# Where the last up sum of two feed-forward columns is kept: in its PSUM bank or in SBUF

## The chip, the core and the metric

The kernel runs on one core of one Trainium2 chip. The metric is the time of one execution on the device, in microseconds (us); of several runs the median is taken. One execution more was taken with the hardware profiler, and all views quoted here are of such executions. The engines are called PE (TensorE, the matmuls), DVE (VectorE), ACT (ScalarE), POOL (GpSimd) and SP (SyncE, which issues the DMAs).

## What is computed

The reference is two layers of cross attention and a feed-forward part each, on x of 8 x 128 tokens and 512 features. The change lies in the last feed-forward part, a gated one with quantised weights:

```python
gate_proj = dequantize(gate_w, gate_s, gate_z, GROUP_SIZE, dt)   # 512 x 1792
up_proj = dequantize(up_w, up_s, up_z, GROUP_SIZE, dt)           # 512 x 1792
down_proj = dequantize(down_w, down_s, down_z, GROUP_SIZE, dt)   # 1792 x 512
gate = jax.nn.silu(jnp.dot(x, gate_proj))
up = jnp.dot(x, up_proj)
return jnp.dot(gate * up, down_proj)
```

`dequantize` subtracts a zero point and multiplies by a scale; both are given for each group of 128 rows and each column. x is normalised before this part, and its result is added to x.

## The kernel before

**The columns.** The 1792 inner features are cut into 14 columns of 128. The list ORDER (line 1089) gives their order: 5, 1, 6, 2, 7, 3, 8, 4, 9, 10, 11, 12, 13, 0. The 1024 tokens are two halves of 512. For columns 0 to 4 the first half of the gated product has been computed ahead, in the layer before, so that only the second half is left here: their instructions are 512 wide, those of the others 1024.

**One column.** Gate and up each have four units (`unit`, line 990), one for each group of 128 rows. A unit is matmuls on PE into a tile f of the PSUM pool `ps_f`, then one instruction that multiplies f by the group's scale and adds it to a sum. [...] The first unit of a sum is a scaled copy on ACT (line 1001). The others are a `scalar_tensor_tensor` on DVE (L1010: the tile `gate` or `up` in SBUF gets f times the scale plus itself). One up unit is different: the fourth, where the whole sum is kept in one tile (`one`, line 1022; all columns but the first three of ORDER). It goes to L1003, which writes the finished sum into f itself, in PSUM, and returns f. In the first three columns the up sum is made of two sums in SBUF, which POOL adds (L1036), and the product reads it there.

Then come `silu` on ACT (L1042), the gated product on DVE (`gated`, L1047: th gets th times the up sum), a rounded copy h_h on ACT (`cast`, L1054) and the remainder h_l = th - h_h (`rest`, L1061). The remainder is made by POOL, in column 0 by DVE (`late`, line 1012). PE multiplies h_l and h_h by the down weights: four units for each column, whose results are summed in `acc`. Such a sum is either L1010 on DVE, or a scaled copy to a tile tmp on ACT (L1007) and an add of two SBUF tiles on POOL (L1008).

**What sets the order.** Most of the kernel is ordered by a scheduler. For the feed-forward part line 1094 (`emit`) gives the program order of a column, and the down units of a column are written among the gate and up units of the next. The last stretch, from line 1122 on, is under `manual_schedule`: on PE, DVE, ACT and POOL the written order is kept. It begins with the product of column 13, the last but one of ORDER; the eight gate and up units of column 0 follow, with the down units of column 12 among them, then the product, cast and remainder of column 0, the down units of column 13, the transposes that turn `acc` back (`turn`, L1159), and the last down units. The fourth up unit of column 13 is still emitted by the loop (line 1120). Each engine takes its instructions in order, and a unit on PE waits until a buffer of `ps_f` is free, that is until the last reader of the tile that held it is done. For an up sum kept in f this last reader is the product.

## Time and profile before

| what | value |
|---|---|
| median of 3 runs | 840.97 us (840.44 to 841.06) |
| the profiled execution | 839.52 us |
| its span, from the first instruction to the last | 837.7 us |
| granted TensorE clock | 1.000 of full speed |
| busy over the span | PE 820.4, DVE 629.9, POOL 598.4, ACT 516.9 us |
| DVE from 797 to 809 us | 11.04 of 12.00 us busy |
| DVE from 809 us to the end | 20.37 of 29 us busy |
| POOL from 809 us to the end | 23.01 of 29 us busy |
| L1047 with the up sum in PSUM | 11 times, 1.21 to 1.22 us (1024 wide), 0.68 to 0.69 us (512 wide) |
| L1047 with the up sum in SBUF | 3 times, 1.61 and 2.17 us (1024 wide), 0.68 us (512 wide) |

Lines of the views read so: start in us, length in us, engine, source line, operation, output<-inputs by the program's names, shapes (partitions x elements), how many were merged; in square brackets the idle time before it and what ended it. In the chain of work that ended last, each piece is start, length and what ran; "issue" is time in which the engine waited for nothing that the profile shows, or, where two instructions overlap in the records, the part of the earlier one that the chain does not follow.

### The profile page before, as it was taken

How to read it: one execution, taken by the hardware profiler on the slowest of the kernel's cores; microseconds unless marked ns; L12 is line 12 of the kernel's file. 1: busy time of each engine (PE TensorE's matmuls, PEld its weight loads, DVE VectorE, ACT ScalarE, POOL GpSimd, SP SyncE). 2: the span in 40 equal slices, each digit the busy share in tenths (PEclk: the TensorE clock that was granted, in tenths of full speed). 3: DMA queues.
4: the chain of work that ended last, by engine and by line, in shares of the span. 5: the costliest groups of instructions: out<-in, count | busy, mean ns of one | idle time of the engine just before them, and what ended most of it. 6: DMA issues, size and time to landing. Idle time of an engine off the chain costs nothing.

```text
span 837.7 us, 14168 instructions
## 1 busy us (share of the span) xinstructions
PE 820.4 (98%) x4312; PEld 694.1 (83%) x4312; DVE 629.9 (75%) x1061; ACT 516.9 (62%) x1694; POOL 598.4 (71%) x612
## 2 busy tenths in 40 slices
PE   7999999999999999999999999999999999999996
PEld 6889998898888888888888888888888877778774
DVE  6805897675777777777777777776798888998996
ACT  6524442245667766776767767676777778665663
POOL 3713882235678888878878778798886678787797
PEclk9999999999999999999999999999999999999999
DMA  9523532173888888898889888888976512221202
GB/s 320 131 69 107 184 114 88 59 240 134 277 248 283 285 280 270 268 282 284 263 271 287 253 279 271 295 265 264 290 241 227 182 58 82 87 84 63 63 27 100
DMA packets 153564, 164.96 MB, mean 197 GB/s; under 512 B 15632, under 2 KB 94224, under 8 KB 153488
## 3 DMA queue, kind: packets, MB, share of 16 engines
q1 hardware_dynamic: 153488, 164.06, 61.2%
q8 instruction: 34, 0.56, 0.3%
q14 instruction: 42, 0.34, 0.1%
HBM read 104.78 MB, written 59.24 MB: 196 GB/s over the span
## 4 chain that ended last, share of the span: by engine, by line
PE 85%; DVE 6%; issue 4%; POOL 3%; ACT 1%; DMA 0%; DVEq 0%; SPq 0%; POOLq 0%; ACTq 0%
PE mm L78 9%; PE mm L80 9%; PE mm L79 9%; PE f L996 7%; PE f L997 7%; PE s L575 7%; PE o L644 6%; PE o L647 6%; PE o L645 6%; PE kv L78 3%; PE kv L80 3%; PE kv L79 3%; PE o L623 2%; PE o L624 2%; PE o L625 2%
## 5 line engine op out<-in xcount | busy, mean ns | idle before, releaser
L589 ACT ACTIVATE pr<-s,nm 128x128 f32<-128x128 f32 x256 | 90.4, 364 | 47.3 <-DVE nm L583 47.1
L616 POOL TENSOR_TENSOR pT_l<-pT,pT_h 128x512 fp32r<-128x512 f32 x64 | 82.9, 1295 | 34.8 <-ACT pT_h L615 23.1
L78 PE MATMUL mm<-wq_l,xnT_h 128*128 128x512 f32 x256 | 105.6, 412 | 0.2 <-DVE q L544 0.2
L80 PE MATMUL mm<-wq_h,xnT_l 128*128 128x512 f32 x256 | 101.2, 395 | 0.0
L79 PE MATMUL mm<-wq_h,xnT_h 128*128 128x512 f32 x256 | 100.7, 393 | 0.0
L644 PE MATMUL o<-wo_l,aT_h 128*128 128x512 f32 x256 | 100.1, 391 | 0.1
L645 PE MATMUL o<-wo_h,aT_h 128*128 128x512 f32 x256 | 99.7, 389 | 0.0
L601 DVE STREAM_TRANSPOSE pb<-pr 128x512 f32<-128x512 f32 x64 | 45.5, 711 | 52.6 <-POOL pr L597 52.6
L597 POOL TENSOR_TENSOR pr<-pr,rs 128x512 f32<-128x512 f32 x64 | 67.9, 1060 | 21.5 <-DVE rs L595 21.2
L535 ACT ACTIVATE junkq<-mm 128x128 f32<-128x128 f32 x256 | 71.6, 280 | 10.9 <-PE mm L80 4.8
L78 PE MATMUL kv<-wkv_l,cT_h 128*128 128x256 f32 x256 | 73.6, 288 | 0.0
L80 PE MATMUL kv<-wkv_h,cT_l 128*128 128x256 f32 x256 | 72.9, 285 | 0.0
L79 PE MATMUL kv<-wkv_h,cT_h 128*128 128x256 f32 x256 | 72.9, 285 | 0.0
L615 ACT CAST pT_h<-pT 128x512 fp32r<-128x512 f32 x64 | 39.8, 622 | 51.7 <-DMA pT<-p_d 50.4
L575 PEld LDWEIGHTS s<-kT,qT 128*128 128x128 f32 x512 | 66.9, 191 | 5.2
L647 PE MATMUL o<-wo_h,aT_l 128*128 128x512 f32 x256 | 69.0, 391 | 0.0
L673 POOL TENSOR_TENSOR qT<-qT,q 128x512 fp32r<-128x512 f32 x42 | 54.0, 1287 | 20.1 <-ACT qT L672 20.1
L366 POOL TENSOR_TENSOR rrq<-msq,nhalf 128x4 f32<-128x4 f32 x64 | 64.5, 1007 | 5.3
L575 PE MATMUL s<-kT,qT 128*128 128x128 f32 x512 | 67.4, 275 | 0.0
L644 PEld LDWEIGHTS o<-wo_l,aT_h 128*128 128x128 f32 x256 | 48.1, 188 | 11.3 <-issue 0.9
L80 PEld LDWEIGHTS mm<-wq_h,xnT_l 128*128 128x128 f32 x256 | 48.1, 188 | 11.0
L629 ACT CAST aT_h<-o 128x512 fp32r<-128x512 f32 x64 | 37.4, 585 | 31.4 <-PE o L625 31.1
(251 smaller groups left out, 2486.8 us busy)
## 6 DMA issues: line engine op xcount, KB each, us to landing
q_d<-qb SPq DMA_DIRECT2D x64, 256.0 KB, 4.3
qT<-q_d SPq DMA_DIRECT2D x64, 256.0 KB, 4.3
p_d<-pb SPq DMA_DIRECT2D x64, 256.0 KB, 2.5
pT<-p_d SPq DMA_DIRECT2D x64, 256.0 KB, 4.5
wst<-in_qpT SPq DMA_DIRECT2D x36, 256.0 KB, 4.2
wst<-in_opT SPq DMA_DIRECT2D x36, 256.0 KB, 3.1
wkv<-in_kvT SPq DMA_DIRECT2D x8, 512.0 KB, 4.0
v_d<-vh SPq DMA_DIRECT2D x16, 256.0 KB, 2.1
```

What stands on the lines that cost most here:

```text
L78: nc.tensor.matmul(o, ah, bl, start=start, stop=False)
L79: nc.tensor.matmul(o, ah, bh, start=False, stop=False)
L80: nc.tensor.matmul(o, al, bh, start=False, stop=stop)
L366: nc.gpsimd.tensor_tensor(r[:, :n], ms[:, :n], nhalf[:, :n], ALU.pow)
L535: nc.scalar.activation(junk, qps[u][:, r * HD : (r + 1) * HD], AF.Square, accum_out=ssq[:, r : r + 1])
L575: nc.tensor.matmul(sp[:, r, :], qTs[u][:, r, :], kTt[blocks[j]][:, :, i, :], start=True, stop=True)
L589: nc.scalar.activation(pr[:, r, :], sps[u][:, r, :], AF.Exp, bias=nms[u][:, r : r + 1], accum_out=sm[:, r : r + 1])
L597: nc.gpsimd.tensor_tensor(pr, pr, rs.unsqueeze(2).to_broadcast([P, NQ, P]), ALU.mult)
L616: nc.gpsimd.tensor_tensor(pl, tps[u], f32(ph), ALU.subtract)
L644: nc.tensor.matmul(po, ah[:, r, :], wl, start=r == 0, stop=False)
L645: nc.tensor.matmul(po, ah[:, r, :], wh, start=False, stop=False)
L647: nc.tensor.matmul(po, al[:, r, :], wo[wset[j], r][0], start=False, stop=r == NREP - 1)
```

## The change

The condition that sends an up unit to L1003 gets one more clause:

```diff
         upf[c] = unit(
-            "P" if one and (m, g) == ("up", KT - 1) else "V", wfs[m], g, lambda hf: (xn2[hf][0][:, g, :], xn2[hf][1][:, g, :]),
+            "P" if one and (m, g) == ("up", KT - 1) and c not in ORDER[-2:] else "V", wfs[m], g, lambda hf: (xn2[hf][0][:, g, :], xn2[hf][1][:, g, :]),
             s_sb[:, c, g : g + 1], gu[m, a], g == a, (1,) if c < NE else (0, 1),
         )
```

In columns 13 and 0 the fourth up unit is now L1010 like the second and third: it writes the sum into the tile `up` in SBUF. `unit` returns nothing, so `gated` (L1047) takes its up operand from `up` and not from f. The nine other columns with one up sum keep L1003. The order of instructions on each engine is the same before and after; two instructions of DVE have another output, two another second input, and the bank of f is released by the sum and no longer by the product.

## The prediction

> **What bounds the kernel where the change acts.** I read four views, in this order. First the page's fourth part, the chain that ended last: over the whole span it is TensorE's (PE).

> ```profile
> PE 85%; DVE 6%; issue 4%; POOL 3%; ACT 1%; DMA 0%; DVEq 0%; SPq 0%; POOLq 0%; ACTq 0%
> ```

> A mean over 837.7 us says little of the last 30. So, second, the same chain piece by piece from 797 us on. Its columns are start, length and what ran.

> ```profile
> 811.22 1.29 DVE f L1003
> ...
> 812.61 0.09 DVE th L1047
> ...
> 813.75 0.76 DVE gate L1010
> ...
> 820.01 0.77 DVE f L1003
> ...
> 820.87 0.70 DVE th L1047
> ...
> 821.59 0.63 ACT h_h L1054
> ...
> 822.24 0.70 DVE h_l L1061
> 822.95 2.55 POOL acc L1008 x2
> 825.54 0.78 PE f L1159 x5
> ```

> Up to 810.0 us the chain is PE's; from there to 821.57 it is VectorE's (DVE), with both gated products (L1047) in it, and then it runs through ScalarE (ACT), DVE and GpSimd (POOL) into the output. Third, DVE's timeline: from 811.22 to 821.56 its eleven instructions have durations of 1.284, 1.221, 0.746, 0.750, 0.750, 1.274, 0.741, 1.274, 0.740, 0.758 and 0.689, 10.23 us in 10.34. DVE is full there, so what is added to one of its instructions arrives at the end, and what is taken from PE does not. Fourth, the timeline of POOL beside DVE, for what runs while the two products run:

> ```profile
> 812.57 2.38 POOL L1008 TENSOR_TENSOR acc<-acc,tmp 128x1024 f32<-128x1024 f32 x1
> 812.61 1.22 DVE L1047 TENSOR_TENSOR th<-th,f 128x1024 f32<-128x1024 f32 x1
> ...
> 819.84 2.38 POOL L1008 TENSOR_TENSOR acc<-acc,tmp 128x1024 f32<-128x1024 f32 x1
> ...
> 820.87 0.69 DVE L1047 TENSOR_TENSOR th<-th,f 128x512 f32<-128x512 f32 x1
> ```

> Both products run beside a POOL add on SBUF operands and neither notices: one operand is f, in PSUM.

> **The change, part by part.** It replaces no instruction by more or fewer. In columns 13 and 0 the last up sum goes from L1003 (into f) to L1010 (into up), and L1047 reads up. The order on all five engines stays, SP's and its DMAs' with it.

> (1) *The sum itself.* L1003 takes 1.284 us for 1024 columns and 0.751 for 512; L1010 into up 1.281 and 0.747. The gap from the sum to the product that needs it is 0.11 us (811.22 + 1.28 to 812.61), and between two dependent sums into up, in SBUF, it is 0.10 (806.918 + 1.284 to 808.307). Cost: 0.

> (2) *The PSUM bank.* f comes free when the sum ends and no longer when the product ends. PE waited for the products twice, 1.4 us in all:

> ```profile
> PE f L996 <- DVE th L1047: 1.4, 2, 0.7
> ```

> Both go. The third gate sum's matmuls would follow the second's (812.81 + 0.23) at about 813.0 rather than 813.89, but DVE reaches them only at 815.45; behind them PE waits at 814.55 for the bank of the second gate sum, which DVE releases. At 821.71 PE's next step, 822.85, waits for ACT's tmp, behind the same product. So late next is DVE in the one case and ACT in the other, and the gain is 0. Its bounds are 0, and 1.4 us if DVE were not full.

> (3) *The product's second operand.* Now both operands are in SBUF. Before has three such products, in columns 5, 1 and 6. The short one ran while POOL was idle, a long one while POOL was not:

> ```profile
> 699.62 0.68 DVE L1047 TENSOR_TENSOR th<-th,up 128x512 f32<-128x512 f32 x1
> ...
> 709.80 1.32 POOL L1036 TENSOR_TENSOR gate<-gate,gate 128x512 f32<-128x512 f32 x1
> 710.03 2.17 DVE L1047 TENSOR_TENSOR th<-th,up 128x1024 f32<-128x1024 f32 x1
> ```

> Undisturbed it costs what the PSUM form costs (0.68 against 0.69), so the floor of this part is 0. The disturbed one ended at 712.20, 1.08 after POOL's add (711.12); alone the form would take 1.22. So DVE stood until POOL was 0.14 short of its end, then ran whole. The other long one, at 696.34, gives 697.95 - 696.88 = 1.07. A third row, in the next fence, agrees: 686.35 + 1.77 = 688.12, 0.55 after POOL's 687.57, and 0.55 = 0.69 - 0.14. It goes the other way too: POOL's 512 add at 696.82, behind the product that ended at 697.95, took 2.29 instead of 1.30 and ended 1.16 after it, 1.30 - 0.14. I take it as a rule of this trace: of a DVE operation with two SBUF inputs and a POOL operation on SBUF, whoever is first runs alone, the other starts 0.14 before its end.

> [...]

> *Who is first at 812.6?* The POOL add starts at 812.57 and the product asks at 812.61; neither start depends on the change. So POOL leads by 0.04 us. The nearest rows: POOL won with a lead of 0.07,

> ```profile
> 686.28 1.29 POOL L1086 TENSOR_TENSOR h_l<-the,h_h 128x512 fp32r<-128x512 f32 x1
> 686.35 1.77 DVE L740 TENSOR_TENSOR the<-the,qb 128x512 f32<-128x512 f32 x1 [1.18 <-ACT gate L1001]
> ```

> and DVE won with a lead of 0.01 (L66 at 107.35 took its 0.40, POOL's L62 at 107.36 took 1.55 instead of 1.29). The lead of 0.04 is nearer to the row that POOL won, so I take POOL as first.

> Then the first product ends at 814.95 + 1.08 = 816.03, not 813.83: **+2.20**. Queued behind it on DVE, without a gap, are three gate sums, two down sums and three up sums, then the second product: all 2.20 later. ACT's cast (813.87) waits for the product, POOL's remainder (L1061, 814.99) for the cast, and POOL's next two adds follow it: 817.19, 819.57, 822.04. The second product asks at 820.87 + 2.20 = 823.07, while POOL's second add runs from 822.04 to 824.42. It stands again and ends at 824.42 + 0.55 = 824.97, not 821.56: **+3.41**. From there the chain in the second fence has no slack: cast, remainder, two POOL adds, transposes, output. The remainder (822.24) already has two SBUF inputs and a free POOL, as before. Sum: 0 + 0 + 3.41.

> The profiled execution took 839.52 us (span 837.7 and 1.8 around it); it would take 842.9. The median of the runs, 840.97, lies 1.45 above that execution; the same 3.4 on it gives **844.4 us**. Bounds of the unknown cost: 0 if POOL is never in the way, and 2 x (2.38 - 0.14) = 4.5 us, 845.5, if each product stood for a whole add.

> **Rivals.**
> (a) *DVE takes the first collision*, because a start in the trace is not quite the moment of the claim. For it: the lead is only 0.04. Then the first product is on time and POOL's add ends at 813.83 + 2.24 = 816.07. POOL's remainder, first and second add follow at 816.02, 818.39 and 820.74, back to back. The second product asks at 820.87, now 0.13 behind, and stands until 823.12: it ends at 823.67, +2.11. That gives 843.1. If DVE won this as well, POOL's add would end at 823.80 and the remainder, asking at 822.24, at 824.35 rather than 822.94: +1.4, 842.4.
> (b) *Nothing moves*: the POOL adds leave the product alone, both last 1.22 and 0.69, and PE's waits were hidden anyway. For it: both products are covered in before. Against it: five rows in (3). 841.0.
> (c) *Faster*: PE's waits were the limit, not DVE. Then the two 0.69 us of (2) and the 0.44 behind the second (PE at 822.85) go, 1.8 us: 839.2. It decides only if DVE has slack of that size between 811.22 and 821.56; the sum above leaves 0.11, so this is nearly excluded.

> **How the numbers follow.** Forecast 55%, (a) 28% with one collision lost and 6% with none, (b) 7%, (c) 2%, and 2% for more than the forecast. The time is the forecast's, 844.4. The range leaves out (b) and (c): from the lower case of (a), 842.4, to 845.2, which is the forecast and most of the way to the upper bound of 845.5. A measurement of this kernel can tell about 0.2% from no change, 1.7 us, so slower begins at 842.65. Forecast, first case of (a), the excess and half of its second case make 88% for slower; the other half and (b) make 10%; (c) is 2%.

> **What would show it.** Right: L1047 near 812.61 lasts about 3.4 us and ends 1.08 after a POOL add; L1047 near 823.1 lasts about 1.9; L1003 is gone from the last two columns; PE's two waits for th are gone from the list of waits and the span is 3.4 longer all the same. For (a): the first L1047 lasts 1.22, the POOL add beside it 3.5, and the second L1047 2.8. Wrong: both products at 1.22 and 0.69, or an end that moves less than the second product does; then there was slack behind DVE that I have not seen.

## The result, and the profile after

The changed kernel takes 847.94 us (median of six runs, 846.11 to 850.86); the kernel before took 840.8 beside it. The ratio is 1.0084 [1.0059, 1.011], that is 5.0 to 9.2 us more, where 3.4 were forecast and 4.2 were the end of the range. The profiled execution took 850.86 us with a span of 849.1.

That execution is the slowest of the six, and it is already 5.17 us late (816.39 against 811.22) where the changed stretch begins, although the program up to there is the same. Such a drift came with the kernel before's own program too: at the same point the other profiled executions of this study stand at -0.3 (e8) to +6.0 us (e6) against before, and the program of e6 up to there is that of before. One profile, of e2, was of a disturbed execution and was taken again (e9). Profiles are compared by their **tail**: from the start of column 13's last up sum to the end of the span. Before: 837.73 - 811.22 = 26.51 us. After: 849.08 - 816.39 = 32.69, 6.18 more. (The spans of the tails are taken from the traces to two decimals; the views show one.)

The chain that ended last, the first view, is of no use here. Its shares over the whole span:

```profile
PE 70%; DVE 8%; POOL 6%; DMA 6%; issue 6%; ACT 3%; SPq 1%; DVEq 0%; POOLq 0%; ACTq 0%
```

PE's share fell by 15 points, from some 712 to some 594 us, where the two spans differ by 11.4: the chain takes another way far ahead of the change, through waits for DMAs from 223 us on that before's chain does not have. What the change did has to be read from its own stretch. The timeline of DVE in the changed kernel:

```profile
816.39 1.28 DVE L1010 SCALAR_TENSOR_TENSOR up<-f,su_sb,up 128x1024 f32<-128x1024 f32 x1
817.77 3.41 DVE L1047 TENSOR_TENSOR th<-th,up 128x1024 f32<-128x1024 f32 x1
...
826.37 1.28 DVE L1010 SCALAR_TENSOR_TENSOR acc<-f,sd_sb,acc 128x1024 f32<-128x1024 f32 x1 [0.96 <-PE f L997]
...
829.67 2.01 DVE L1047 TENSOR_TENSOR th<-th,up 128x512 f32<-128x512 f32 x1
832.37 0.69 DVE L1061 TENSOR_TENSOR h_l<-th,h_h 128x512 fp32r<-128x512 f32 x1 [0.69 <-ACT h_h L1054]
```

and that of POOL (x3 stands for three adds merged, of which the last is the one beside the first product):

```profile
814.00 6.10 POOL L1008 TENSOR_TENSOR acc<-acc,tmp 128x1024 f32<-128x1024 f32 x3
...
828.75 2.38 POOL L1008 TENSOR_TENSOR acc<-acc,tmp 128x1024 f32<-128x1024 f32 x1 [1.69 <-ACT tmp L1007]
```

The sum lasts what it lasted, and the product follows it after 0.10 us. The first product takes 3.41 us for 1.22 and ends at 821.18, 1.08 after POOL's add (820.10). The second takes 2.01 for 0.69 and ends at 831.68, 0.55 after POOL's add (831.13). So both products stood behind POOL, as forecast. But 2.19 and 1.32 are 3.51 of the tail's 6.18. Between the products DVE now waits for PE (the row at 826.37: 0.96 us), where before it had no such wait. The rest shows on PE, in its timeline:

```profile
821.90 0.50 PE L996 MATMUL f<-h_l,wf_down 128*128 128x512 f32 x1 [3.08 <-DVE gate L1010]
824.36 0.63 PE L996 MATMUL f<-h_l,wf_down 128*128 128x512 f32 x1
...
832.98 0.50 PE L996 MATMUL f<-h_l,wf_down 128*128 128x512 f32 x1 [2.58 <-ACT tmp L1007]
```

PE stood for 3.08 and 2.58 us, and soon after the first stand matmuls took 0.63 us, where those of before take 0.39 to 0.40 (from 816.55 to 818.84 us, at full clock). The same time cut into stretches says why. Columns: stretch, its length, busy us (and count) of PE, PE's weight loads, DVE, ACT and POOL, the granted TensorE clock, DMA share, GB/s:

```profile
819.87:823.28 3.41, 1.38 (x6) 1.04 (x6) 3.20 (x4) 2.06 (x2) 1.17 (x2) 1.00 0.00 0
823.28:826.70 3.42, 3.42 (x10) 2.69 (x9) 2.46 (x4) 1.21 (x3) 3.42 (x2) 0.50 0.00 0
...
830.11:833.52 3.41, 0.83 (x4) 0.30 (x2) 2.73 (x3) 1.79 (x3) 1.48 (x2) 1.00 0.00 0
833.52:836.94 3.42, 3.42 (x11) 2.70 (x11) 2.02 (x4) 1.37 (x2) 3.42 (x4) 0.50 0.00 0
```

Twice PE was idle for most of a stretch of 3.41 us (2.03 and 2.58), and in the stretch behind it the clock was 0.50. In the profile of before the clock is 1.00 until 0.7 us before the end of the span, when PE has long been done. The tail's 6.18 us fall into four parts: first product +2.19; from its end to the start of the second, 8.49 for 7.04 us, +1.45; second product +1.32; from its end to the end of the span, 17.40 for 16.17, +1.22 (and -0.01 ahead of the first).

**Theory A**: the forecast's collisions are there, and by making DVE late they make PE idle so long that its clock falls to half, twice, for 1.45 and 1.22 us. **Theory B**: the clock is a by-product without a price, and the missing 2.7 us come from somewhere else in the changed columns (the drift ahead, another wait). A third question is whether anything but POOL's adds is at work at all.

### The profile page after: what moved, and what is told of

It is laid out like the page before. It is cut to its first block, busy times and chain, and to the rows that moved or that the text cites. A ratio compares the mean times of both kernels' runs of the same rounds, so it can differ in the third digit from the quotient of the medians.

```text
span 849.1 us, 14167 instructions
## 1 busy us (share of the span) xinstructions
PE 824.5 (97%) x4312; PEld 696.4 (82%) x4312; DVE 632.9 (75%) x1061; ACT 517.5 (61%) x1694; POOL 598.7 (71%) x612
## 4 chain that ended last, share of the span: by engine, by line
PE 70%; DVE 8%; POOL 6%; DMA 6%; issue 6%; ACT 3%; SPq 1%; DVEq 0%; POOLq 0%; ACTq 0%
PE f L996 8%; PE f L997 7%; PE mm L78 7%; PE mm L80 7%; PE mm L79 7%; PE o L644 5%; PE o L647 5%; PE o L645 5%; PE s L575 5%; DMA pT<-p_d 3%; PE kv L78 2%; PE kv L80 2%; PE kv L79 2%; DMA q_d<-qb 2%; PE o L623 1%
## 5 line engine op out<-in xcount | busy, mean ns | idle before, releaser
L1008 POOL TENSOR_TENSOR acc<-acc,tmp 128x1024 f32<-128x1024 f32 (+1 forms) x23 | 49.4, 2160 | 13.1 <-ACT tmp L1007 11.0
```

## The experiments

### e3: PE kept busy

The changed kernel, in which two units on PE repeat their matmuls into the same tile just where PE stood. Nothing else is changed.

```diff
...
+            for _ in range(1 + again):
-            nc.tensor.matmul(ps[:, hf, :], w, rl, start=True, stop=False)
-            nc.tensor.matmul(ps[:, hf, :], w, rh, start=False, stop=True)
+                nc.tensor.matmul(ps[:, hf, :], w, rl, start=True, stop=False)
+                nc.tensor.matmul(ps[:, hf, :], w, rh, start=False, stop=True)
...
+            6 if (m, g, c) == ("gate", 3, ORDER[-1]) else 0,
...
+            5 if (o, c, hs) == (2, ORDER[-2], (0,)) else 0,
```

> The changed kernel, with the last gate unit of column 0 multiplied six times more and one down unit of column 13 (third of its first half) five times more, into the same bank with the same result: 22 matmuls that fill 2.7 and 2.3 us of PE's two long waits and wait for nothing. Theory A: both products last as in the changed kernel, 3.4 and 1.9 us, but the clock stays at full speed; the tail is 26.5 + 2.2 + 1.2 = 29.9 us, 2.8 less than in the changed kernel, although PE does more; time 3.4 over before, about 844. Theory B (the 2.8 us are not the clock's): the tail stays at 32.7 or grows by the added matmuls.

Measured: 844.57 us beside 841.02 of before, ratio 1.0037 [1.002, 1.0054], and a tail of 29.98 (841.41 - 811.43), 3.47 longer than before's. With 22 matmuls more the kernel is 3.4 us nearer to before than the changed one (median against median). DVE's timeline and two stretches of e3 (the product is L1049 there):

```profile
812.82 3.46 DVE L1049 TENSOR_TENSOR th<-th,up 128x1024 f32<-128x1024 f32 x1
...
823.31 1.91 DVE L1049 TENSOR_TENSOR th<-th,up 128x512 f32<-128x512 f32 x1
```

```profile
811.40:824.00 12.60, 12.21 (x52) 9.09 (x52) 12.08 (x12) 5.08 (x6) 10.22 (x6) 1.00 0.05 17
824.00:841.00 17.00, 10.82 (x58) 7.76 (x57) 9.99 (x14) 5.42 (x9) 10.65 (x9) 1.00 0.34 124
```

Both collisions are there in full, the clock is 1.00, and DVE's last instruction ends 3.47 later than in before. This is the forecast's case as it was worked out (3.41), and it speaks for A: what lies above it goes with the clock. The mean granted clock of the runs says the same beyond the one profile. One step of 3.41 us at half takes 0.0020 off the mean of such a span, and its end, where PE has nothing left to do, took 0.0004 (before) and 0.0011 (after). The six runs of the changed kernel have 0.997 once, 0.995 four times and 0.993 once: one, two and three such steps. The twelve of e3 have 0.998 to 1.000, so at most one each, and eight of them, at 0.999 or 1.000, none.

### e1, e2, e9: each column alone

The new clause for one column only: in e1 for column 13, in e2 and e9 (the same program) for column 0.

```diff
-... and c not in ORDER[-2:] else "V"
+... and c != ORDER[-2] else "V"
```

> The last up sum goes to SBUF in column 13 alone; column 0 keeps it in f. Compared is the tail, from the start of column 13's last up sum to the end of the span: 26.5 us in the kernel before (811.22 to 837.7), 32.7 in the changed one (816.39 to 849.1). Theory A (the product and POOL's adds exclude each other, and the long wait that this makes on PE lets the granted TensorE clock fall to half for one window): the first product lasts 3.4 us, +2.2; PE then idles some 3.2 us and the clock falls once, +1.4; the second product lasts 0.69. Tail about 30.1, time some 3.6 over before. Theory B (the products are slower by the lock, but the rest of the loss, 2.8 us, comes from elsewhere: PE running ahead on the freed bank, or the weights): no drop of the clock here, tail 28.7. Theory C (the loss belongs to column 0): tail 26.5.

> The last up sum goes to SBUF in column 0 alone; column 13 keeps it in f. The tail is 26.5 us in the kernel before, 32.7 in the changed one. Theory A: the first product lasts 1.22; the second asks at the time it had before, one us into POOL's add of 2.38, and lasts 1.9, +1.2. PE, with its bank free early, then waits some 2.8 us for ACT's tmp; if the granted clock falls for that, +1.3 more. Tail 27.7 without the fall, 29.0 with it; time 1.2 to 2.5 over before. Theory B (PE running ahead on the freed bank costs by itself): the loss is there without a drop of the clock. Theory C (the loss belongs to column 13): tail 26.5.

> The last up sum goes to SBUF in column 0 alone, once more, for its profile. Theory A, as sized by the runs so far: the first product lasts 1.22; the second asks at 9.64 us from the start of column 13's last up sum, beside the POOL add of 8.62 to 11.00, lasts about 1.9 and ends near 11.5 (10.34 before), +1.2; PE then waits 2.5 us, from about 10.4 to 12.9. The clock falls only if a window of 3.41 us holds about two thirds of that wait: the end is 1.2 later than before, or about 2.5.

Measured for column 13 alone: 845.13, ratio 1.0042 [1.0024, 1.0059], tail 31.32 (+4.81). The product takes 3.417 us, 2.20 more, so 2.61 are left. Its stretches:

```profile
816.36:819.78 3.42, 1.19 (x6) 0.67 (x4) 3.32 (x2) 0.00 (x0) 2.40 (x2) 1.00 0.00 0
819.78:823.19 3.41, 2.56 (x6) 2.08 (x7) 2.67 (x5) 2.06 (x2) 2.12 (x1) 0.50 0.00 0
823.19:826.60 3.41, 3.41 (x9) 2.64 (x9) 2.03 (x3) 1.21 (x2) 2.60 (x2) 0.50 0.00 0
```

After a stretch with 2.23 us idle the clock fell, and behind the next one, which still had 0.85 idle, it stayed down for one more. Expected were 30.1 by A and 28.7 by B; A had one stretch at half clock in it.

For column 0 alone: 843.09, ratio 1.0014 [0.9999, 1.0029], not clear of no change. The profile is e9's: tail 28.89 (+2.38). The product takes 1.915 us (+1.23), and DVE's last instruction ends 2.36 later, of which 1.14 come after the product. The mean clock of this profile is 0.997, which by the numbers above is one step at half and the end of the span. That last part does not come in every execution: of the twelve other runs of e2 five have 0.997 too (843.25 to 845.39 us), while four have 0.999 (841.16 to 843.09) and so no step at half clock. The limit that was expected at two thirds of a wait of 2.5 us lies, by the runs, between 1.78 (e4, no fall) and 1.86 us of a step (e11, a fall). The two columns' parts do not add up (4.81 + 2.38 against 6.18): e1's and e9's profiles have three steps at half clock between them, that of the changed kernel two.

### e6, e7: without the two adds

Two POOL adds, of down units (3, 11) and (2, 12), the ones beside the products, are left out: in e6 of the kernel before, in e7 of the changed one.

```diff
...
-            nc.gpsimd.tensor_tensor(dst, dst, a2, ALU.add)
+            if not leave:
+                nc.gpsimd.tensor_tensor(dst, dst, a2, ALU.add)
...
+            (o, c) in ((3, ORDER[-4]), (2, ORDER[-3])),
```

> The kernel before without the two POOL adds that run beside the two products (down sums of column 11, third unit, and column 12, fourth unit, are not added to acc). This is the base for the next run. All theories: the products last 1.22 and 0.69, as before, and POOL has pauses in place of the adds; POOL's last four adds start as before, after the remainder of column 0. Time as before, 841, or up to 0.5 less.

> The changed kernel without the same two POOL adds. Theory A (the whole loss is the exclusion by these two adds and what follows from it): both products last 1.22 and 0.69, PE's waits for the products are gone, the clock stays, and the time is that of the base run within 0.3 us: the early release of the bank is worth nothing, since DVE is full. Theory B (the change costs by itself, by its operands or by PE running ahead): several us over the base remain. Theory C (PE's two waits were worth something): 0.7 to 1.4 us below the base.

Measured: e6 841.68, 1.0012 [0.9996, 1.0029], tail 26.51; e7 841.4, 0.9998 [0.9983, 1.0013], tail 26.52. DVE's products in e7:

```profile
816.86 1.23 DVE L1048 TENSOR_TENSOR th<-th,up 128x1024 f32<-128x1024 f32 x1
...
825.11 0.69 DVE L1048 TENSOR_TENSOR th<-th,up 128x512 f32<-128x512 f32 x1
```

Without these two adds the change neither costs nor gains: the whole difference hangs on the two collisions, and the bank that comes free early gains nothing (the two tails differ by 0.02 us).

### e8: POOL busy, but not reading

The changed kernel, in which the two adds are replaced by memsets of tmp.

```diff
...
-            nc.gpsimd.tensor_tensor(dst, dst, a2, ALU.add)
+            if leave:
+                nc.gpsimd.memset(a2, 0.0)
+            else:
+                nc.gpsimd.tensor_tensor(dst, dst, a2, ALU.add)
```

> The changed kernel with the same two POOL adds replaced by POOL memsets of the same 1024 columns into tmp, which write SBUF and read nothing (the sums are not added to acc). The first memset is under way when the first product asks. Theory A1 (only POOL's reading excludes the product): both products last 1.22 and 0.69, the time is that of the run without the adds. Theory A2 (any POOL instruction on SBUF excludes it): the first product waits for the rest of the memset, some 0.5 to 1.0 us, and the end moves with it.

Measured: 840.13, 0.999 [0.998, 1.0], tail 26.52. The timeline of POOL and DVE:

```profile
812.12 0.95 POOL L1009 MEMSET tmp<- 128x1024 f32 x1
812.29 1.23 DVE L1050 TENSOR_TENSOR th<-th,up 128x1024 f32<-128x1024 f32 x1
...
819.52 0.95 POOL L1009 MEMSET tmp<- 128x1024 f32 x1
```

The product starts 0.17 us after the memset, runs beside it for 0.78, and takes its 1.23. This POOL instruction, which only writes SBUF, does not hold it up; the adds, which read it, do (3.41 us in the profile after). The second memset had run 0.95 us and ended at 820.47, before the product came at 820.55.

### e4, e5: POOL made late

If the first add comes after the first product, DVE should win and POOL stand, the rival (a) of the prediction. A small POOL instruction ahead of the add is to make it late: 128x1 in e4, 128x128 in e5.

```diff
...
+            if late_add:
+                nc.gpsimd.tensor_tensor(fa.tile([P, 1], F32, name="gap"), a2[:, 0, 0:1], a2[:, 0, 0:1], ALU.add)
```

> The changed kernel with one POOL instruction of one column added ahead of the POOL add that starts 0.04 us before the first product, so that this add comes some 0.1 to 0.2 us later and after the product. Theory A, with the order of asking deciding: the first product lasts 1.22 to 1.4, the POOL add 3.5; POOL's next three follow late, the last of them from about 0.1 before the second product asks, so that this one lasts 2.8; the tail is 26.5 + 2.1 = 28.6, and 29.9 if PE's one long wait (3.5 us) lets the clock fall. The changed kernel has 32.7. Theory B (the slow product is not a matter of who is first, but of sharing): the first product lasts 3.4 as in the changed kernel and the tail stays at 32.7.

> As the run before it, with a longer POOL instruction in front (128 columns, some 0.45 us), so that the POOL add cannot start before the first product asks. Times are from the start of column 13's last up sum. Theory A (whoever asks first runs alone, and the one who waits comes next): the first product asks at 1.38, waits at most for the short instruction and lasts 1.2 to 1.3; the POOL add beside it lasts 3.3 to 3.5 and ends near 4.9; POOL's next three follow without a pause, the last starts near 9.5, just ahead of the second product (9.70), which therefore lasts 2.8 and ends near 12.5 (10.34 in the kernel before). The end comes 2.1 later than before, 3.5 if PE's wait of some 3.4 us lets the clock fall; time 843.1 to 844.5. Theory B (a product with two SBUF inputs is slow beside POOL whoever is first): the first product lasts 3.3 again and the end stays 5 to 6 later.

e4 did not do what it was for: the add came 1.263 us after the start of the up sum, where it comes 1.35 after it in the kernel before, so POOL won again and the product took 3.327. It took 848.53, 1.0077 [1.0055, 1.01], tail 31.39. It is of use for another reason. In its profile PE's second stand is spread over two stretches, so that this one follows the first fall:

```profile
826.54:829.96 3.42, 1.64 (x7) 0.98 (x6) 2.76 (x2) 0.46 (x1) 2.38 (x1) 1.00 0.00 0
829.96:833.37 3.41, 2.61 (x11) 1.65 (x11) 2.98 (x5) 2.70 (x5) 2.52 (x3) 1.00 0.00 0
```

With 1.78 us idle the clock stayed at 1.00. The wait of PE is as long as in the changed kernel (2.58), and the tail is 1.30 shorter, close to the 1.22 that stood behind the second product. So it is not the wait itself that costs this part.

e5 did do it. POOL's timeline (the two lines ahead) and DVE's:

```profile
814.76 0.39 POOL L1009 TENSOR_TENSOR gap<-tmp 128x128 f32<-128x128 f32 x1
815.12 3.37 POOL L1010 TENSOR_TENSOR acc<-acc,tmp 128x1024 f32<-128x1024 f32 x1
```

```profile
814.91 1.33 DVE L1049 TENSOR_TENSOR th<-th,up 128x1024 f32<-128x1024 f32 x1
...
823.26 2.82 DVE L1049 TENSOR_TENSOR th<-th,up 128x512 f32<-128x512 f32 x1
```

The first product takes 1.33 us, the add beside it 3.37, and the second product 2.82, in place of 0.69: +2.13, as rival (a) had it (2.11). The time, though, is 846.0, 1.0055 [1.004, 1.007], tail 31.05, and not 843.1 to 844.5: of the 4.54 us by which the tail is longer than before's, 2.41 lie behind the second product's 2.13. There DVE waits 0.71 and 0.96 us for PE (at 829.48 and 831.19), in before once 0.25, and the mean clock of the profile is 0.995, as in the profile after, which has two steps at half. So the order of the two engines decides where the collision's price falls, and the clock is added either way.

### e10, e11: a version that beats both?

The opposite direction: in the kernel before, column 0's product too is kept in PSUM (written into f), so that the cast and the remainder read it there and the remainder no longer has two SBUF operands. In e10 two down sums are moved behind the product besides.

```diff
...
-        nc.vector.tensor_tensor(part(th, c), part(th, c), part(gu["up", 0], c) if up is None else up, ALU.mult)
+        inf[c] = up if c == ORDER[-1] else part(th, c)
+        nc.vector.tensor_tensor(inf[c], part(th, c), part(gu["up", 0], c) if up is None else up, ALU.mult)
...
-        nc.scalar.copy(part(hh, c), part(th, c))
+        nc.scalar.copy(part(hh, c), inf[c])
...
-        late(c).tensor_tensor(part(hl, c), part(th, c), part(f32(hh), c), ALU.subtract)
+        late(c).tensor_tensor(part(hl, c), inf[c], part(f32(hh), c), ALU.subtract)
```

and in e10 alone:

```diff
-        downs("V")
...
-        downs("VA")
+        down_unit(2, ORDER[-3], eng="A")
...
-        down_unit(0, ORDER[-2], (0,), "A")
+        down_unit(1, ORDER[-3], eng="V")
...
+        down_unit(3, ORDER[-3], eng="V")
+        down_unit(0, ORDER[-2], (0,), "A")
```

> The kernel before, carried the other way: in column 0 the product itself is written into f, so that the cast and the remainder (DVE, L1062 here) read it from PSUM and no DVE instruction of the tail but that of the unchanged column 13 has two SBUF inputs; and on DVE the two down sums of column 12 (1.27 each) stand behind the product of column 0 and no longer ahead of it. If DVE was the limit from 811 to 821 us and POOL had room, the second product ends some 2 us earlier, POOL's adds close up by its pause of 0.7 us, and the tail is 25.7 to 25.9 us where the kernel before has 26.5; the ratio is 0.999, under what the runs can tell. If the remainder still stood for POOL's add, the tail stays at 26.5.

> The kernel before with the first half of the last edit alone: the product of column 0 is written into f, in PSUM, and the cast and the remainder read it there; the order is that of the kernel before. The remainder no longer excludes POOL, so POOL's next add can start some 0.08 us earlier, when its tmp is there: tail 26.4 where the kernel before has 26.5. If POOL's add waited for its tmp alone, no difference.

e10: 842.28 beside 841.68, 1.0004 [0.9989, 1.0019], tail 26.34 where 25.7 to 25.9 were expected. Its remainder on DVE (L1062) beside POOL:

```profile
823.95 0.68 DVE L1062 TENSOR_TENSOR h_l<-f,h_h 128x512 fp32r<-128x512 f32 x1
```

POOL's adds of SBUF operands run from 820.11 to 826.10 (three, merged in the view), and the remainder, with one operand in PSUM, took its 0.68 beside them. The product ended 1.47 us earlier than in before, but the end of DVE moved by 0.17 only: the last down sum ahead of the output's transposes starts no earlier (14.05 us after the start of column 13's last up sum, 13.98 before) and waits for PE. That the gain was lost there is read from the waits; no run tested it.

e11, without the moved sums, took 843.21 in one run, tail 28.16 where 26.4 was expected. The bank is held longer, until the remainder has read it (it ends at 825.01, 1.40 us behind the end of the product), and PE pays:

```profile
822.65:826.07 3.42, 1.56 (x7) 0.96 (x6) 2.51 (x5) 1.76 (x3) 2.66 (x2) 1.00 0.00 0
826.07:829.48 3.41, 3.41 (x13) 2.72 (x12) 1.95 (x3) 1.37 (x2) 3.41 (x4) 0.50 0.00 0
```

1.86 us idle in one stretch, and the clock falls (in before the stretch around this product has 1.13). Neither version is measurably better than before.

## Why the prediction was wrong

**The sum (1)** cost nothing, as said: 1.28 us, and 0.10 to the product.

**The bank (2).** That PE's two waits for the products go, and that this gains nothing, held: e7, which has this part and no collision, has before's tail to 0.02 us. Rival (c) is out by the same run. The 0.11 us of slack that spoke against it was too little: the eleven durations overlap, and a view of the same 10.34 us has DVE busy for 9.82; the rest is mostly gaps of some 0.1 us ahead of instructions that need the result before them.

**The second operand (3).** Held in mechanism and size. POOL won the first collision with a lead of 0.031 us (forecast 0.04); the first product got 2.19 longer (2.20), the second 1.32 in the profile after and 1.22 in e3 (1.21 by the ends of 3.41 and 2.20). "From there the chain has no slack" held as well: in e3, 3.46 us on the products arrived as 3.47 at DVE's end and in the tail. In the profile after itself the second collision is partly luck: POOL's add had waited 1.69 us for tmp and the product asked 1.4 us later than forecast, both behind the slow clock, and they met all the same. Rival (a) was described rightly, as e5 shows, but the order did not fall that way. Rival (b) is out by e7 and e8, in which the products do run at 1.23 and 0.69, and only there.

**The step that failed** is in (2) and in the bounds of (3): PE was taken as an engine whose waiting is free. The working says that what is taken from PE does not arrive at the end, and that the gain of its shorter waits is 0; from this it passed over what *longer* waits do to it. The first product, 2.2 us late, keeps DVE from freeing PE's banks: behind column 0's last gate unit PE stands 3.08 us, until DVE has read the first of the three gate sums (`ps_f` is opened with four buffers, line 981). The second holds up the cast and tmp, and PE stands 2.58. Each time its clock then was 0.50, and PE, which had slack until then, became the engine that the others wait for. In the profile after, this term is 1.45 + 1.22 = 2.67 us of tail; e3, which takes it away alone, gives 2.71 (32.69 - 29.98). The term had no place in the sum and none in "2 x (2.38 - 0.14) = 4.5 us", which was thought to be the most that the change could cost.

How far before stands from it can be read in the same view of the kernel before, cut at the steps of its clock:

```profile
813.15:816.56 3.41, 2.72 (x12) 1.84 (x12) 3.20 (x5) 2.38 (x3) 3.37 (x2) 1.00 0.00 0
...
819.97:823.39 3.42, 2.29 (x9) 1.11 (x8) 2.59 (x4) 1.78 (x3) 2.70 (x2) 1.00 0.00 0
```

Around the two products PE is idle for 0.69 and 1.13 us of a step. The least after which a view of these runs has the clock fall is 1.86 (e11), so there was room for 1.2 and 0.7 us more, which products that end 2.2 and 3.4 us late could fill. Before's own profile gives this limit only loosely: a step with 1.78 us idle had no fall behind it, one with 3.41 (PE has nothing left to do there) had. And the steps do not keep their place against the program: the first one that begins after the start of column 13's last up sum begins 0.07 us behind it in after, 1.24 in e1, 1.93 in before and 2.02 in e4.

**What stays open.** The medians differ by 7.1 us and the tails of the profiles by 6.18. The 1.0 us between them lies within the interval (5.0 to 9.2). The mean clocks tell how many steps an execution ran at half clock, not where they lay; where was seen in single profiles only. The drift ahead of the tail is not explained. In the profile after, some 3.5 of its 5.2 us arise between 210 and 260 us, with a wait of PE of 2.5 us that before does not have, and most of the rest between 530 and 630. The wait of 2.5 us falls into two steps, from 236.19 and 239.61 us, in which PE was idle for 1.05 and 1.43 us, and the clock stayed at 1.00. e6's profile has a mean clock of 0.997 and before's tail, so the step at half clock that this mean stands for lies ahead of the tail.

## What to carry to other kernels

Before an operand moves from PSUM to SBUF in a DVE instruction with two tensor inputs, look in POOL's timeline for what reads SBUF beside it: a product of 1.22 us stood 2.19 behind an add of 2.38. And price a stall by who waits behind it, engines with slack included: a wait that PE can afford as time can still cost it its clock, so add up PE's idle time in stretches of 3.41 us before and after, and where one would come to the 1.86 us that were enough here (e11), count the 1.1 to 1.5 us that such a step cost here (1.14 in e9, 1.22 and 1.45 in the profile after) on top, or give PE something to do there, as e3 did.

## What the runs showed of the hardware that was not expected

PE's gaps in the profile after were 3.08 and 2.58 us, each shorter than one step of 3.41, and the clock fell both times; in e4 2.58 us of idle time, 1.78 in one step and 0.80 in the next, had no fall behind them. It is the idle share of a fixed step that counts in these rows.

A lead of 0.031 us (after) was enough for POOL to take the whole first collision (the product took 3.41); with DVE first by 0.2 (e5) it was DVE (1.33). And an fp32 product of two operands lasts nearly the same from SBUF where POOL does not read, 1.23 and 0.69 us (e7, e8), as from PSUM, 1.22 and 0.69 (before).
